# Four engines in a written order in front of the first attention of a convolution and attention network

## Chip, cores and metric

The kernel runs on one core of a Trainium2 chip. The metric is the device time of one execution in microseconds; the time before is the median of 13 executions. Engines are named as the profile names them: PE (TensorE), ACT (ScalarE), DVE (VectorE), POOL (GpSimd) and SP (SyncE, which here only issues DMAs).

## What is computed

The reference is a network of several layers on an image of 256 channels and 64 x 64 places: a windowed linear attention, a deformable convolution, a second attention, a mixture of experts, a third attention and a second mixture of experts. The change touches only the first layer. Cut to what matters:

```python
q = sigmoid(einsum(x, Wq)); k = sigmoid(einsum(x, Wk)); v = einsum(x, Wv)   # 8 heads of 32 channels
v = v / max(norm(v, axis=1), 1e-12)
Ik  = _integral(k)                       # sums over all rows above and columns to the left
Ikv = _integral(einsum('bfhw,bghw->bfghw', k, v))
for w in (1, 2, 4):                      # windows of 64, 32, 16 places
    ws = 64 // w
    wk, wkv = _box(Ik, ws), _box(Ikv, ws)          # sums in a window around each place
    attn = einsum('bdhw,bdfhw->bfhw', q, wkv)
    norm = einsum('bdhw,bdhw->bhw', q, wk)
    outs.append(attn / (norm + 1e-6))
out = einsum(concat(outs), Wout) + bout
```

`x` stands here for the image after a group normalisation (32 groups of channels); the layer's result is added to the image itself.

## The kernel before

**The stage.** `layer0` (L331) takes the image `xc`, normalises it into `y` (`group_norm`, L157) and works in two halves of 128 channels, that is four heads each. For each half three functions prepare what the attention itself (`half0`) needs: `project0` (L400), `sums0` (L445) and `norms0` (L475). The 4096 places lie in 8 blocks of 512 (8 rows of the image); a block holds 8 tiles of 8 x 8 places, and in `y`, `q` and `k` the tiles of a block follow one another.

**`project0`** makes k and then q for all 8 blocks: two matmuls of 512 columns a block into a PSUM tile `l_qk_ps` (three buffers) and a sigmoid on ACT into `l_k` or `l_q` (L408). Then, block by block, it makes keys and values with places in partitions: 8 matmuls into two tiles `l_kv_ps` (four buffers); ACT takes the sigmoid of the keys into `l_kt` (L423) and the squares of the values into `l_sq` (L425); DVE adds the squares of a head (L426) and bounds the sum (L427); ACT takes the square root (L428), for which it loads another table and then the first one again; DVE inverts it (L429) and scales the values (L432). The values go to DRAM (`l_vd`, L433). Then come the tile sums, for each 8 x 8 tile the sum of key times value: 8 matmuls of a 64 x 128 stationary and 128 columns into two `l_S_ps` tiles (they share the buffers of `l_qk_ps`), of which only the four 32 x 32 squares on the diagonal are wanted; ACT copies each square by itself into `l_S` (L443), eight copies a block.

**`sums0`** runs on POOL (all at L449) when all blocks of `l_S` are there: pairs of neighbouring tiles, `l_near` (sums of three rows of pairs), and sums over seven neighbouring tiles in columns (`l_R`) and then in rows (back into `l_S`). The results go to DRAM as `l_neard` and `l_fard`.

**`norms0`** makes the normalisers. ACT copies k into a raster `l_T` (L485), DVE takes a running sum along each row of a block (L486, with `gate` as a reset at each row's start) and then adds rows and blocks (L487), so that `l_T` holds the integral of k. For each block and window, DVE subtracts two stretches of rows (L502, `l_d`), ACT copies the left edge (L504), DVE subtracts columns (L506 and L508, `l_e`) and multiplies by q (L510, `l_prq`, three buffers); PE adds over the channels of a head (L515, `l_nrm_ps`, with `head_at`); at the end DVE adds 1e-6 and inverts (L517, L518), and the result goes to DRAM (`l_recd`).

**What sets the order.** The order of each engine's instructions in this stage is chosen by a scheduler from the dependencies and its own estimates; only in the attention that follows is PE's order the written one (`manual_schedule` with PE alone). Every engine and the SP queue work strictly in that order: an instruction that waits holds up all behind it. A tile pool gives a tag a number of buffers, and who writes a buffer waits for all readers of what it held.

**Then attention.** `vt` (values with the places of a column strip in partitions) is loaded from `l_vd` by `tall` (L375), half of it through SP's and half through ACT's queue; its space was that of the prepared stage, so it waits for the last `l_nrm_ps` matmul. `bd` (L382) are block-diagonal states, cleared by POOL and filled from `l_fard` and `l_neard` (L530). The first matmuls of attention are `l_s` (L657); they need a strip of k (`l_kc`, L551).

Of the kernel before, what the change touches and what calls it, by code (L numbers as in the profile page):

```python
# [10 lines left out]
F32 = mybir.dt.float32  # L11
# [77 lines left out]
class Net:  # L89
# [145 lines left out]
    def consts0(self, pool):  # L235
# [8 lines left out]
        self.gate = pool.tile([P, TR, HW], F32, tag="gate", name="gate")  # L244
# [86 lines left out]
    def layer0(self, xc, x, xd, done):  # L331
# [4 lines left out]
        with tc.tile_pool(name="l0", bufs=1) as pool, tc.tile_pool(name="l0d", bufs=1, space=DRAM) as dpool:  # L336
# [9 lines left out]
            with tc.tile_pool(name="l0y", bufs=1) as ypool:  # L346
                self.consts0(ypool)
# [5 lines left out]
                with (  # L353
                    tc.tile_pool(name="l0g", bufs=1) as gpool,
                    tc.tile_pool(name="l0a", bufs=2) as wp,
                    tc.tile_pool(name="l0a_ps", bufs=2, space=PSUM) as ps,
                ):
                    self.weights(ypool, ["w_qk0", "w_kv0"])
                    for hf in range(2):
                        S = gpool.tile([P, NBLK, NU, D], F32, tag="S", name="l0_S")  # L360
                        self.project0(hf, y, q[hf], k[hf], None if hf else v, vd[hf], S, wp, ps)
                        self.sums0(S, fard[hf], neard[hf], gpool)
                        self.norms0(q[hf], k[hf], recd[hf], gpool, wp, ps)
            with (
# [6 lines left out]
                def tall(hf):  # L371
                    by_rows = vd[hf].rearrange("(i b j) (h n) c -> b n i j h c", b=2, j=4, h=2)
                    for b in range(2):
                        for i in range(4):
                            (nc.sync, nc.scalar)[b].dma_start(  # L375
                                out=vt[b * HW : (b + 1) * HW, i].rearrange("p (j h) c -> p j h c", h=2), in_=by_rows[b][:, i])
# [4 lines left out]
                for b in bd[0] + bd[1]:  # L381
                    nc.gpsimd.memset(b, 0.0)  # L382
# [16 lines left out]

    def project0(self, hf, y, q, k, v, vd, S, wp, ps):  # L400

        nc, w = self.nc, self.w
        for dst, base in ((k, C), (q, 0)):
            cols = slice(base + hf * P, base + hf * P + P)
            for nb in range(NBLK):
                p = ps.tile([P, NB], F32, tag="qk", name="l0_qk_ps", bufs=3)
                self.mm(p, [(w["w_qk0"][:, kt, cols], y[:, kt, nb * NB : (nb + 1) * NB]) for kt in range(2)])
                nc.scalar.activation(dst[:, nb * NB : (nb + 1) * NB], p, AF.Sigmoid)  # L408
        cols = slice(hf * 2 * P, (hf + 1) * 2 * P)
        for nb in range(NBLK):  # L410
            ts = slice(nb * TPB, (nb + 1) * TPB)
            vb = wp.tile([P, TPB, P], F32, tag="vb", name="l0_vb") if v is None else v[:, ts, :]
            kt4 = wp.tile([P, TPB, P], F32, tag="kt", name="l0_kt")
            ss = wp.tile([P, TPB, 4], F32, tag="ss", name="l0_ss")
            sq = wp.tile([P, TPB, 4, D], F32, tag="sq", name="l0_sq")
# [12 lines left out]
            nc.scalar.activation(ss, ss, AF.Sqrt)  # L428
            nc.vector.reciprocal(ss, ss)  # L429
# [3 lines left out]
            nc.sync.dma_start(out=vd[ts].rearrange("t p c -> p t c"), in_=vb)  # L433

            sums = [ps.tile([P, TPB, P], F32, tag="qk", name="l0_S_ps", bufs=3) for _ in range(2)]
            for i in range(TPB):
                for b, p in enumerate(sums):
                    half = slice(b * HW, (b + 1) * HW)
                    self.mm(p[:, i, :], [(kt4[half, i, :], vb[half, i, :])])
            for b, p in enumerate(sums):  # L440
                for h in range(4):
                    hp = slice(h * D, (h + 1) * D)
                    nc.scalar.copy(S[hp, nb, b::2, :], p[hp, :, hp])  # L443

    def sums0(self, S, fard, neard, pool):  # L445


        nc = self.nc
        add = lambda o, a, b: nc.gpsimd.tensor_tensor(o, a, b, ALU.add)  # L449
        pairs = pool.tile([P, NBLK, 4, D], F32, tag="pairs", name="l0_pairs")  # L450
# [2280 lines left out]
```

## Time and profile before

| what | us |
|---|---|
| median of 13 runs (3566.31 to 3579.47) | 3574.62 |
| the profiled execution's own time | 3573.69 |
| its span, first to last instruction | 3571.6 |
| first projection matmul (`l_qk_ps`) starts | 34.95 |
| last addition of the first half's integral (L487) starts | 66.25 |
| last normaliser matmul (`l_nrm_ps`) of the second half starts | 274.83 |
| first attention matmul (`l_s`) starts | 294.18 |

The mean granted clock of PE is 0.946. In the profile's rows a line is given with the engine, the operation, the tile written and those read, shapes as partitions x elements, and in square brackets the idle time before it and what ended it. A matmul in 32-bit floats leaves two records, so 8 matmuls in the code are 16 in the trace. A merged row gives the time from the first of its instructions to the end of the last.

### The profile page before, as it was taken

The page shows a single profiled execution, that of the slowest core. Times are in us where ns is not written, and L with a number is a line of the kernel's source. Part 1 is how long each engine was busy: PE and PEld are TensorE (multiplying, and loading weights), DVE is VectorE, ACT ScalarE, POOL GpSimd, SP SyncE. Part 2 cuts the span into 40 slices and gives each one's busy share as a digit, 9 for nine tenths or more (in the row PEclk, how much of TensorE's full clock was granted, in tenths as well). Part 3 has the DMA queues.
Part 4 walks back from the last instruction along what each step waited for, and adds up shares of the span by engine and source line. Part 5 has one row for each costly group of instructions (what it writes and reads, how often), then busy time and mean ns, then how long its engine had stood idle before and what let it go on. Part 6 is the DMA issues. An engine that isn't in the chain of part 4 may idle for free.

```text
span 3571.6 us, 64097 instructions
## 1 busy us (share of the span) xinstructions
PE 3175.8 (89%) x24636; PEld 2355.9 (66%) x24636; DVE 2314.2 (65%) x5296; ACT 1357.8 (38%) x2681; POOL 1503.0 (42%) x1336
## 2 busy tenths in 40 slices
PE   5867999999996899797877979999999996999997
PEld 3332444444444888765665747888888885898986
DVE  6784666667764677797445566777777775555552
ACT  4553333344334666342332344222222221333331
POOL 1336777788862555443233435000000002555552
PEclk9978999999998999898878989999999997999998
DMA  1115755721115222200117854223332323555554
GB/s 68 35 42 111 175 146 152 188 70 51 51 51 174 61 74 73 56 1 1 37 41 240 258 207 154 89 97 99 99 97 88 95 89 123 184 189 210 195 200 185
DMA packets 241424, 406.87 MB, mean 114 GB/s; under 512 B 78097, under 2 KB 152594, under 8 KB 231634
## 3 DMA queue, kind: packets, MB, share of 16 engines
q1 hardware_dynamic: 212658, 345.19, 31.1%
q0 software_dynamic: 13056, 35.93, 2.6%
q10 hardware_dynamic: 15392, 21.52, 1.9%
q8 instruction: 198, 3.24, 0.4%
q14 instruction: 120, 0.98, 0.1%
HBM read 287.07 MB, written 111.30 MB: 112 GB/s over the span
## 4 chain that ended last, share of the span: by engine, by line
PE 39%; DVE 7%; issue 6%; DMA 5%; POOL 3%; ACT 2%; SPq 0%; POOLq 0%; DVEq 0%; ACTq 0%
PE a_sa_ps L2354 6%; PE f_h_ps L146 5%; PE a_oa_ps L2393 3%; PE a_ob_ps L2393 3%; PE a_oc_ps L2393 3%; DMA ys<-f_y,f_at 3%; PE a_sb_ps L2354 3%; PE f_ya_ps L146 2%; PE f_yb_ps L146 2%; POOL ys L2109 1%; PE a_od_ps L2393 1%; PE l_acc_ps L1048 1%; PE a_q_ps L146 1%; PE a_sc_ps L2354 1%; PE a_s L1544 1%
## 5 line engine op out<-in xcount | busy, mean ns | idle before, releaser
L664 ACT COPY l_sc<-l_s 128x384 f32<-128x384 f32 (+1 forms) x632 | 303.6, 532 | 469.7 <-PE l_s L657 445.9
L669 DVE TENSOR_TENSOR l_sm<-l_s,mask 128x256 f32<-128x256 f32 (+2 forms) x628 | 308.1, 551 | 95.5 <-PE l_s L657 94.6
L1922 POOL DMA_INDIRECT xs<-f_room,f_to x64 | 64.7, 1012 | 699.9 <-issue 586.9
L146 PE MATMUL f_h_ps<-f_xT,f_w 128*128 128x256 f32 x1440 | 341.2, 388 | 18.8 <-ACT f_h L2039 8.1
L146 PEld LDWEIGHTS f_h_ps<-f_xT,f_w 128*128 128x128 f32 x1440 | 262.3, 192 | 83.3 <-ACT f_h L2039 21.5
L657 PE MATMUL l_s<-l_q,l_k 32*128 32x256 f32 (+3 forms) x2944 | 272.1, 454 | 0.1
L2373 ACT ACTIVATE a_e<-a_e 128x512 f32<-128x512 f32 x256 | 155.9, 629 | 245.8 <-DVE a_e L2343 231.2
L674 POOL TENSOR_TENSOR l_sm<-l_sc,mask 128x768 f32<-128x768 f32 (+1 forms) x116 | 202.5, 1753 | 87.8 <-ACT l_sc L664 87.6
L2039 ACT ACTIVATE f_h<-f_h_ps,f_w 128x256 f32<-128x256 f32 x360 | 166.3, 470 | 187.3 <-PE f_h_ps L146 177.2
L1044 DVE TENSOR_TENSOR l_pr<-l_vk,l_w_ps 128x1280 f32<-128x1280 f32 x128 | 186.6, 1481 | 56.1 <-PE l_acc_ps L1048 38.0
L657 PEld LDWEIGHTS l_s<-l_q,l_k 32*128 32x128 f32 x2944 | 133.1, 184 | 116.2 <-issue 67.9
L1048 PE MATMUL l_acc_ps<-ident,l_pr 128*128 128x128 f32 x1600 | 198.8, 278 | 8.7 <-POOL l_pr L1039 8.5
L2109 POOL DMA_INDIRECT ys<-f_y,f_at x144 | 146.0, 1014 | 138.8 <-ACT f_y L2108 88.6
L1048 PEld LDWEIGHTS l_acc_ps<-ident,l_pr 128*128 128x128 f32 x1600 | 185.4, 144 | 15.5 <-POOL l_pr L1039 10.4
L678 POOL TENSOR_TENSOR l_sm<-l_sc,mask 128x256 f32<-128x256 f32 (+1 forms) x220 | 185.2, 871 | 23.5 <-ACT l_sc L664 22.6
L2066 POOL TENSOR_TENSOR f_wt<-f_w 128x512 f32<-128x512 f32 x72 | 89.9, 1269 | 218.3 <-PE f_ya_ps L146 206.1
L2354 PE MATMUL a_sa_ps<-a_q,a_kt 128*128 128x256 f32 x512 | 156.5, 387 | 16.4 <-DVE a_u L2359 15.4
L2358 ACT COPY a_u<-a_sa_ps 128x256 f32<-128x256 f32 x128 | 47.6, 372 | 293.5 <-PE a_sa_ps L2354 289.3
L703 PE MATMUL l_b_ps<-l_sm,l_v 128*32 128x256 f32 (+2 forms) x2176 | 154.1, 374 | 0.0
L2354 PE MATMUL a_sa_ps<-a_qt,a_kt 128*128 128x256 f32 x512 | 152.7, 380 | 0.0
L674 POOL TENSOR_TENSOR l_sm<-l_sc,mask_c 128x768 f32<-128x768 f32 (+1 forms) x64 | 120.0, 1894 | 34.6 <-ACT l_sc L664 34.1
L2354 PE MATMUL a_sb_ps<-a_qt,a_kt 128*128 128x256 f32 x512 | 131.4, 379 | 0.0
(549 smaller groups left out, 7477.6 us busy)
## 6 DMA issues: line engine op xcount, KB each, us to landing
a_kt<-a_kd SPq DMA_DIRECT2D x128, 512.0 KB
f_w<-in_f_w SPq DMA_DIRECT2D x36, 1152.0 KB
f_w<-in_f_w SPq DMA_DIRECT2D x36, 1028.0 KB
xs<-zero SPq DMA_DIRECT2D x8, 4160.0 KB
l_vk<-vt SPq DMA_DIRECT2D x180, 128.0 KB
f_x<-xs SPq DMA_DIRECT2D x72, 260.0 KB
f_w<-in_f_w SPq DMA_DIRECT2D x36, 384.0 KB
l_rcp<-l_recd SPq DMA_DIRECT2D x48, 256.0 KB
```

Source lines behind the costliest of these rows:

```text
L146: self.nc.tensor.matmul(out, lhsT, rhs, start=(i == 0), stop=(i == len(pairs) - 1))
L657: nc.tensor.matmul(s[pair, j][:, at : at + m, :], key(hp), qs[hp], start=(z == 0), stop=(z == len(pieces) - 1))
L664: nc.scalar.copy(sc[:, j], s[1, j])
L669: nc.vector.tensor_tensor(to(pair, j, kind, at), pick(s[pair, j], kind, which), mask, ALU.mult)
L674: nc.gpsimd.tensor_tensor(out[:, :, at, :], of[:, :, which, :], bc(mask, 1, 2), ALU.mult)
L678: nc.gpsimd.tensor_tensor(to(1, j, kind, at), pick(sc[:, j], kind, which), mask, ALU.mult)
L1044: nc.vector.tensor_tensor(pr, vk, bc(held["w"][:, j, dy], 3, D), ALU.mult)
L1048: nc.tensor.matmul(acc[:, m, j, :], pf[:, dx, m * P : (m + 1) * P], self.ident, is_transpose=True, start=(j == 0 and dy == 0 and dx == 0 a ...
L2039: nc.scalar.activation(h[:, m, :], q, AF.Gelu, bias=w1[:, 2 * hidden + m : 2 * hidden + m + 1])
L2109: nc.gpsimd.indirect_dma_start(out=self.ys_parts[(i % 4) * NI + k], in_=y[:, k, :], in_offset=None, out_offset=bass.IndirectOffsetOnAxis(a ...
L2354: mm = lambda out, i, right: nc.tensor.matmul(out, A[i], right, start=True, stop=True)
L2393: nc.tensor.matmul(out, vs[:, j, i, :], right, start=(j == 0 and side != 1), stop=(j == NPAIR - 1 and side != 0))
```

## The change

The three functions are replaced by one, `prep0`, called for each half, and the order of PE, DVE, ACT and POOL inside it is the written one.

- First the 8 k blocks. ACT takes the sigmoid twice out of PSUM, once straight into the raster `l_T` and once into `l_k`; the copy L485 is gone. `l_T`, `gate` and `l_d` get a column of zeros in front (65 instead of 64), so that the subtraction of columns needs no copy of a left edge; L504 is gone. Running sums and the 14 additions follow as before.
- Then, for block b: POOL subtracts rows for windows 64 and 32 (`ahead`; the one for window 16 is made by DVE); PE makes q of block b+1 and keys and values of block b; then what was left *behind* from block b-1 is done: its tile sums and their copies, its running sums on POOL, its normaliser matmuls; then DVE weighs block b by q (`weighed`) and scales its values (`values`). The weighting is written in two parts, of which the first reads the row difference directly.
- A tile sum is made of four matmuls of 64 x 32 stationary and 32 columns, one for each head, so that `l_S_ps` holds only what is wanted and ACT copies it in two pieces.
- The sums over tiles run along with the blocks: the seven neighbours in columns at once, those in rows as a running window over the last blocks. `l_fard` and `l_neard` are written after block 7.
- `vt` is loaded by column strip in 8 DMAs on each queue, strips 4 to 7 first, instead of 4. The first `bd` is cleared by DVE.

The diff, cut to its core:

```diff
-        self.gate = pool.tile([P, TR, HW], F32, tag="gate", name="gate")
+        self.gate = pool.tile([P, TR, HW + 1], F32, tag="gate", name="gate")
...
-                    for hf in range(2):
-                        S = gpool.tile([P, NBLK, NU, D], F32, tag="S", name="l0_S")
-                        self.project0(hf, y, q[hf], k[hf], None if hf else v, vd[hf], S, wp, ps)
-                        self.sums0(S, fard[hf], neard[hf], gpool)
-                        self.norms0(q[hf], k[hf], recd[hf], gpool, wp, ps)
+                    self.consts0(ypool)
+                    T = gpool.tile([P, HW + 1, HW + 1], F32, tag="T", name="l0_T")
+                    nc.gpsimd.memset(T[:, 0, :], 0.0)
+                    nc.gpsimd.memset(T[:, 1:, 0:1], 0.0)
+                    ET = mybir.EngineType
+                    with tc.manual_schedule(engines={ET.PE, ET.DVE, ET.Activation, ET.Pool}):
+                        for hf in range(2):
+                            self.prep0(hf, y, q[hf], k[hf], None if hf else v, vd[hf], fard[hf], neard[hf], recd[hf], T, gpool, wp, ps)
...
-                        for i in range(4):
-                            (nc.sync, nc.scalar)[b].dma_start(
-                                out=vt[b * HW : (b + 1) * HW, i].rearrange("p (j h) c -> p j h c", h=2), in_=by_rows[b][:, i])
+                    for u in (4, 5, 6, 7, 0, 1, 2, 3):
+                        for b in range(2):
+                            (nc.sync, nc.scalar)[b].dma_start(out=vt[b * HW : (b + 1) * HW, :, u], in_=by_rows[b][:, :, u // 2, u % 2])
...
-                    nc.gpsimd.memset(b, 0.0)
+                    (nc.vector if b is bd[0][0] else nc.gpsimd).memset(b, 0.0)
...
+        def channels(dst, nb, base, also=None):
+            p = ps.tile([P, NB], F32, tag="qk", name="l0_qk_ps", bufs=3)
+            cols = slice(base + hf * P, base + hf * P + P)
+            self.mm(p, [(w["w_qk0"][:, kt, cols], y[:, kt, blk(nb)]) for kt in range(2)])
+            if also is not None:
+                nc.scalar.activation(also, p.rearrange("p (u r c) -> p r u c", u=NU, r=TR), AF.Sigmoid)
+            nc.scalar.activation(dst[:, blk(nb)], p, AF.Sigmoid)
...
+            sums = [ps.tile([P, TPB, D], F32, tag="qk", name="l0_S_ps", bufs=3) for _ in range(2)]
             for i in range(TPB):
-                for b, p in enumerate(sums):
-                    half = slice(b * HW, (b + 1) * HW)
-                    self.mm(p[:, i, :], [(kt4[half, i, :], vb[half, i, :])])
+                for h in range(4):
+                    for b, p in enumerate(sums):
+                        half, hp = slice(b * HW, (b + 1) * HW), slice(h * D, (h + 1) * D)
+                        self.mm(p[hp, i, :], [(kt4[half, i, hp], vb[half, i, hp])])
             for b, p in enumerate(sums):
-                for h in range(4):
-                    hp = slice(h * D, (h + 1) * D)
-                    nc.scalar.copy(S[hp, nb, b::2, :], p[hp, :, hp])
+                nc.scalar.copy(S[:, nb, b::2, :], p)
...
+                if i >= ni:
+                    hi, d = d, wp.tile([P, TR, HW + 1], F32, tag="d", name="l0_d", bufs=3)
+                    sub = (nc.vector if ws == 16 else nc.gpsimd).tensor_tensor
...
+                mid = HW - 2 * half
+                if mid > 0:
+                    nc.vector.tensor_tensor(e[:, :, :mid], d[:, :, 2 * half : HW], d[:, :, :mid], ALU.subtract)
+                nc.vector.tensor_tensor(e[:, :, mid:], bc(d[:, :, HW], 2, half), d[:, :, mid : mid + half], ALU.subtract)
                 pr = wp.tile([P, NU, TR, HC], F32, tag="prq", name="l0_prq", bufs=3)
+                nc.vector.tensor_tensor(to[:, :, :ni], wide(d[:, :, half : 2 * half]), q5[:, i, :, :ni], ALU.mult)
+                nc.vector.tensor_tensor(to[:, :, ni:], wide(e), q5[:, i, :, ni:], ALU.mult)
...
+            plus(pair, a[:, 0::2], a[:, 1::2])
+            ends, two = o[:, 0:8:7], o[:, 1:7:5]
+            plus(ends, a[:, 0:5:4], a[:, 1:6:4])
+            plus(two, a[:, 2:7:4], a[:, 3:8:4])
+            plus(ends, ends, two)
+            for u in range(1, 4):
+                plus(o[:, u], o[:, u - 1], a[:, u + 3])
+                plus(o[:, 7 - u], o[:, 8 - u], a[:, 4 - u])
+            if nb > 0:
+                plus(near[:, nb], pairs[:, 0], pairs[:, 1])
...
+            if nb > 1:
+                plus(near[:, nb - 1], near[:, nb - 1], pair)
+                if nb < 7:
+                    plus(S[:, max(0, nb - 3)], S[:, max(0, nb - 4)], o)
...
+            if nb == 7:
+                plus(S[:, 7], last, o)
+                for i in range(6, 3, -1):
+                    plus(S[:, i], S[:, i + 1], R[:, i - 3])
+                nc.sync.dma_start(out=fard, in_=S)
+                nc.sync.dma_start(out=neard, in_=near)
...
+        behind = []
+        channels(q, 0, 0)
+        for nb in range(NBLK):
+            ds = ahead(nb)
+            if nb + 1 < NBLK:
+                channels(q, nb + 1, 0)
+            got = keys(nb)
+            for go in behind:
+                go()
+            prs = weighed(nb, ds)
+            vals = values(nb, *got)
+            behind = [lambda nb=nb, vals=vals: tiles(nb, *vals), lambda nb=nb: sums(nb), lambda nb=nb, prs=prs: norms(nb, prs)]
+        for go in behind:
+            go()
```

## The prediction

> **What bounds the stage now.** I read the page first, then busy time by stage, then the timeline of the stage that the change rewrites. The chain that ended last names no line of this stage among its large shares, so it is read from the timeline.
>
> From the page:
>
> ```profile
> span 3571.6 us, 64097 instructions
> PE 3175.8 (89%) x24636; PEld 2355.9 (66%) x24636; DVE 2314.2 (65%) x5296; ACT 1357.8 (38%) x2681; POOL 1503.0 (42%) x1336
> ```
>
> Busy time by stage (stretch, length, then PE, weight load, DVE, ACT and POOL busy with instruction counts, granted clock, DMA share, GB/s):
>
> ```profile
> 67.00:126.00 59.00, 51.74 (x289) 34.51 (x288) 30.49 (x72) 50.82 (x131) 6.26 (x4) 1.00 0.13 36
> 126.00:165.00 39.00, 32.60 (x62) 9.00 (x61) 35.14 (x45) 9.09 (x22) 22.38 (x20) 0.91 0.10 40
> 165.00:234.00 69.00, 55.11 (x289) 35.64 (x288) 53.00 (x105) 54.92 (x139) 1.26 (x1) 0.95 0.12 34
> 234.00:276.00 42.00, 20.02 (x26) 2.00 (x24) 37.66 (x45) 5.06 (x17) 26.79 (x22) 0.63 0.09 38
> 276.00:294.00 18.00, 0.00 (x0) 0.00 (x0) 3.95 (x2) 0.00 (x0) 3.04 (x5) 0.55 0.92 195
> ```
>
> The bound changes hands. In the first and third rows keys and values run (ACT 86% busy, DVE half idle); in the second and fourth normalisers run (DVE 90%; in the fourth PE is 48% busy at a clock of 0.63). The last row waits for DMA. Inside a key/value block the timeline shows why it takes 6.05 us:
>
> ```profile
> 87.00 0.17 DVE L427 TENSOR_SCALAR l_ss<-l_ss 128x16 f32<-128x16 f32 x1
> 88.26 1.28 ACT L428 ACT_TABLE_LOAD   x1
> ...
> 89.79 1.28 ACT L423 ACT_TABLE_LOAD   x1
> 89.81 0.25 DVE L429 RECIPROCAL l_ss<-l_ss 128x16 f32<-128x16 f32 x1 [2.63 <-ACT l_ss L428]
> 90.16 0.76 DVE L432 TENSOR_TENSOR l_v<-l_kv_ps,l_ss 128x256 f32<-128x256 f32 x2
> ...
> 90.73 1.25 PE L146 MATMUL l_S_ps<-l_v,l_kt 64*128 64x128 f32 x16 [1.15 <-DVE l_v L432]
> ```
>
> DVE waits 2.63 us for a square root that stands behind eight copies of tile sums and a table load. And when POOL adds beside DVE, this happens:
>
> ```profile
> 131.74 5.77 POOL L449 TENSOR_TENSOR l_R<-l_R,l_S 128x256 f32<-128x256 f32 x6
> 132.25 0.82 DVE L508 TENSOR_TENSOR l_e<-l_d 128x248 f32<-128x248 f32 x1
> ...
> 133.20 1.00 DVE L510 TENSOR_TENSOR l_prq<-l_e,l_q 128x512 f32<-128x512 f32 x1
> ...
> 149.16 0.69 DVE L510 TENSOR_TENSOR l_prq<-l_e,l_q 128x512 f32<-128x512 f32 x1
> ```
>
> Six POOL adds and six DVE operations alternate one to one: the same L510 takes 1.00 us beside POOL and 0.69 without. This is the price to watch, for the change puts POOL adds beside DVE in every block.
>
> **The new order, step by step.** Times are from the span's start; DVE operations in a row start 0.08 us closer than their durations.
>
> *Integral of k, half 0.* Before, the twelfth k matmul ends at 42.3 (row at 34.95, 7.38 us). Five more blocks of 4 records at 0.43 us: 50.9. One sigmoid (0.60, now straight from PSUM into T; it replaces the 0.62 copy L485), one scan (1.20), a hand-over of 0.1: 52.7. Then 14 dependent additions L487 at 0.72 (520 instead of 512 elements): 62.9. Before, the last was done at 66.9.
>
> *First block.* Reduce 0.72, maximum 0.12, weighting, reciprocal and two products 1.1 (89.81 to 90.92). Weighting by start-to-start times (256 elements 0.34, 128 0.20, 64 0.13, 384 0.47, 448 0.54): window 64: 3 x 0.34 = 1.0; window 32: 0.34+0.20+0.20+0.47 = 1.2; window 16: 0.47+0.13+0.13+0.54 = 1.3, and from block 1 on its row difference 0.72. Sum 3.5 without, 4.2 with. Block 0: 5.5 us, taken as 5.7 for hand-overs.
>
> *Other blocks.* A new wait closes a loop. PE does q(b+1), keys(b), then tile sums(b-1), normaliser matmuls(b-1). DVE's first weighting of block b needs a buffer of l_prq (three of them) that the normaliser matmuls of b-1 have read; those stand behind tile sums(b-1) on PE, which wait for values(b-1) of DVE. Per turn, from the end of the values: tile sums end 0.8 later (64 records; the nearest row, L690 with 64 records of 32 columns, takes 1.10; they start after the first of two products), normaliser matmuls 1.06 (six records at 110.08), rest of the weighting 3.9, collisions 2.0, reciprocal and products 1.1: **8.9 us**.
>
> Behind PE's wait stand q(b+1), keys(b) and so the ACT chain. They have slack: PE's own work is 4 x 0.43 + 3.72 + 1.1 + 1.06 = 7.6 us a block. ACT's is about 5.0 (two table loads 2.56, five activations 1.6, square root 0.22, two copies of tile sums 0.5 in place of eight at 2.14), and the square root now has the 4 us of weighting to hide in. If that cover went, it would be the old 2.63 us a block.
>
> *Collisions.* POOL's running sums are 13 adds a block, after the two copies, that is just as weighting resumes; behind them on POOL stand the row differences of the next block (10 a half), which fall on DVE's reduce and products, operations with at most one SBUF input. POOL adds take 0.48 (128 elements, L2335 and its neighbours), 0.68 (256), 1.16 (512), hence by the slope 0.36 at 64 and 0.30 at 32. In the rows above a pair takes 0.96; DVE's share is 0.44, so POOL's is 0.52 of its 0.68: 0.16 is hidden. Eleven adds met: 3 x 0.20 + 6 x 0.14 + 2 x 0.32 = 2.0. Ends: 0, if POOL runs in DVE's wait, and 3.9 (all of 3 x 0.36 + 6 x 0.30 + 2 x 0.48).
> The Trainium skill (SBUF — State Buffer, "Who interferes with whom") says that a DVE instruction with two SBUF inputs and a GpSimd instruction that reads SBUF exclude each other for the whole instruction, which speaks against this change. By it the collisions would be 3.9 and the forecast 27 us later; the alternating rows agree in kind and are 0.16 us milder, so I keep 2.0.
>
> *Tile sums.* 64 records of 32 columns replace 16 of 128 (1.25 us). Bounds: 1.10 (L690, 17 ns apart) and 5.0 (the old rows' 78 ns each). I take 1.1: L690 is nearest in stationary width and count.
> The Trainium skill (TensorEngine Tiling (Array Packing), "Instruction Overhead") gives each matmul some 60 cycles and warns against narrowing what is already small. L690 at 17 ns apart says that different array tiles share such a cost; no run here shows this exact tile.
>
> *Sum.* A half is 5.7 + 7 x 8.9 = 68.0. Half 0: 62.9 + 68.0 = 130.9, last tile sums and normalisers 1.9: 132.8. Half 1 starts only there, since PE is in order: 8 k blocks x 1.72 = 13.8, sigmoid, scan and hand-over 1.9, additions 10.1: 158.6. Half 0's reciprocal of 3.35 us on DVE lies beside the k blocks. Then 68.0 and 1.9: **228.5**, against 275.9 before (last L515 row, 274.83 + 1.05). Gain so far 47.4.
>
> *Hand-over to attention.* Before: 275.9 to the first l_s matmul at 294.2, 18.3 us. Now SP has fard and neard of half 1 ahead of its vt loads, and they wait for POOL: copies done at 228.0, 16 adds 7.0 (12 as above, four of 256): 235.0. ACT's half of vt moves meanwhile. Issue times alone (recd and states 0.7, 8 vt at 0.57, w_out 0.63, four bd 2.58, kc 0.66) and the landing of kc (3.1) give 247.3. By bytes: 3.8 MB are left (neard 0.5, fard 1, recd 0.2, vt 1, w_out 0.75, bd 0.13, kc 0.25) where 3.3 MB took 15.2 us plus 3.1: 255.6. I take **252**: nearer to the bytes. So 5 to 6 us of the gain go back. Edits at nothing: the first bd memset on DVE (about 0.5 us; it waits for transfers out of the space that it takes, and behind it on DVE stand the first l_sm products, which need the first l_s matmul anyway); the pads of T and gate; vt of half 1 in eight pieces a queue, with the far jobs of half 0 to hide in, or 0.57 us each on ACT if that cover goes.
>
> Net: 294.2 - 252 = 42 us. The profiled execution took 3573.69 us (2.1 us around its span; median of the runs 3574.62): 3573.7 - 42 = **3532**. Later stages keep their order on every engine.
>
> **Rivals.**
> A, PE is the bound: POOL's adds slip into DVE's wait. The loop falls to PE's 7.6: 14 blocks x 1.3 = 18 less, 3514. For: POOL's small adds leave DVE gaps. Against: sums and weighting are released together.
> B, POOL holds DVE for whole adds: 14 x 1.9 = 27 more, 3559. For: L502 at 1.75 against 0.69 beside larger POOL adds. Against: the 0.16 above.
> C, slower than before: the 64 small matmuls are not shared among array tiles. At the old 78 ns each, tile sums take 5.0 and stand in the loop: 16 x 3.9 = 62 more, 3594. It decides from 42/16 = 2.6 us extra, 58 ns a record. For: the old tile sums' rows. Against: L690.
> D, the order doesn't come out as written, or gains are lost at the hand-over: within 0.2%, 3572. Against: the built order shows PE, DVE, ACT and POOL as written.
>
> **Numbers.** Forecast 0.56, A 0.13, B 0.17, C 0.10, D 0.04. A measurement of this kernel tells 0.2% (7 us) from no change. Range 3509 (A with the hand-over at 247) to 3564 (B with it at 256). Faster 0.85 (forecast, A, most of B), same 0.04, slower 0.11.
>
> **What would show it.** Right: last scan at 52 to 53 and the first reduce at 63; blocks 8.9 us apart; l_nrm matmuls behind tile sums and DVE waiting for them 0.5 to 1 us a block; DVE's L502-like operations stretched while POOL runs; nrm of half 1 done near 228; first l_s matmul near 252. Wrong: tile sums over 2.5 us, blocks over 11, a granted clock below 0.85 with PE 80% busy, or ACT's square root late again.

## The result and the profile after

The changed kernel takes **3521.07 us** (median of 7 runs, 3513.49 to 3530.48) against 3573.98 (31 runs) for the kernel before; the ratio is 0.9855 (95% interval 0.9843 to 0.9867), 53 us less. The forecast was 3532, 42 us less. The profiled execution took 3525.29 us.

Up to the first matmul of attention (`l_s`) the forecast holds almost to the microsecond: 251.49 us where 252 was forecast. The 10 us that are missing from the forecast come after it: the first output projection (`l_x_ps`) starts at 352.7 instead of 405.5, 52.8 us earlier. In this one profile 4 us of that are lost again later (the span is 48.4 shorter); the medians, with 53, do not show this loss.

From the page after:

```profile
span 3523.2 us, 65631 instructions
PE 3133.8 (89%) x25404; PEld 2346.2 (67%) x25404; DVE 2303.5 (65%) x5325; ACT 1318.9 (37%) x2537; POOL 1567.6 (44%) x1523
```

DVE and PE are hardly less busy than before, POOL is busier. What went is waiting, as busy time by stage shows (columns as in the rows of before: stretch, length, PE, weight load, DVE, ACT, POOL, granted clock, DMA share, GB/s):

```profile
35.00:63.00 28.00, 27.74 (x76) 15.04 (x76) 20.70 (x26) 17.18 (x30) 0.30 (x2) 1.00 0.00 0
63.00:130.00 67.00, 47.45 (x640) 28.67 (x640) 61.15 (x136) 34.54 (x70) 53.44 (x99) 0.85 0.11 29
130.00:160.00 30.00, 29.45 (x143) 15.46 (x122) 24.28 (x25) 14.10 (x26) 7.36 (x18) 0.93 0.19 68
160.00:227.00 67.00, 48.02 (x673) 29.20 (x676) 60.37 (x135) 34.81 (x72) 54.45 (x100) 0.84 0.10 29
227.00:245.00 18.00, 1.56 (x6) 0.00 (x0) 4.95 (x3) 0.16 (x1) 8.55 (x21) 0.50 0.92 230
```

The eight blocks of a half are the second and the fourth row. DVE is busy for 91% of them (it was 52% in the key/value stage before), POOL for 80%, PE for 71% at a clock of 0.85. DVE is nearest its limit, but these are means over a half; what holds a single block is read from the timeline.

The timeline of the changed kernel, first in block 0, where POOL does nothing, then in two blocks of the second half of the row (start, duration, engine, line, operation; in brackets the idle time before it and who ended it):

```profile
63.16 0.68 DVE L443 TENSOR_REDUCE l_ss<-l_sq 128x16 f32<-128x512 f32 x1
63.87 0.17 DVE L444 TENSOR_SCALAR l_ss<-l_ss 128x16 f32<-128x16 f32 x1
63.95 0.42 DVE L497 TENSOR_TENSOR l_e<-l_T 128x256 f32<-128x256 f32 x1
64.29 0.42 DVE L500 TENSOR_TENSOR l_prq<-l_T,l_q 128x256 f32<-128x256 f32 x1
...
68.47 0.68 DVE L443 TENSOR_REDUCE l_ss<-l_sq 128x16 f32<-128x512 f32 x1
...
71.12 0.56 DVE L500 TENSOR_TENSOR l_prq<-l_T,l_q 128x256 f32<-128x256 f32 x1 [1.45 <-PE l_nrm_ps L509]
...
93.07 0.75 PE L146 MATMUL l_S_ps<-l_v,l_kt 64*32 64x32 f32 x64 [1.08 <-DVE l_v L454]
...
94.20 0.22 ACT L445 ACTIVATE l_ss<-l_ss 128x16 f32<-128x16 f32 x1 [0.22 <-DVE l_ss L444]
...
95.32 1.49 DVE L497 TENSOR_TENSOR l_e<-l_d 128x256 f32<-128x256 f32 x1 [1.15 <-POOL l_d L478]
...
101.58 0.24 DVE L451 RECIPROCAL l_ss<-l_ss 128x16 f32<-128x16 f32 x1
...
103.24 1.02 DVE L444 TENSOR_SCALAR l_ss<-l_ss 128x16 f32<-128x16 f32 x1
104.27 1.49 DVE L497 TENSOR_TENSOR l_e<-l_d 128x256 f32<-128x256 f32 x1
105.67 0.67 DVE L500 TENSOR_TENSOR l_prq<-l_d,l_q 128x256 f32<-128x256 f32 x1
```

The reader is to see four things. The square root (L445) waits 0.22 us at 94.20, and in other blocks up to 4.2, but always for DVE's own maximum (L444); DVE's reciprocal (at 101.58) waits for it in no block, where it waited 2.63 before. Tile sums take 0.75 us for 64 records. The wait that was forecast, DVE for normaliser matmuls, is there once (at 71.12, block 1). From block 4 on there is another: DVE waits for POOL's row differences `l_d` (1.15 us in blocks 4 and 7), or what runs on DVE beside them is drawn out (L444 1.02 instead of 0.17, L497 1.49 instead of 0.42). In block 5 the long L444 costs nothing by itself: L497 at 104.27 reads the row difference on which POOL works from 103.03 to 104.23, so with a short L444 DVE would have waited for it, as at 95.32. POOL's own timeline tells why:

```profile
94.10 2.43 POOL L478 TENSOR_TENSOR l_d<-l_T 128x520 f32<-128x520 f32 x2
96.49 0.64 POOL L520 TENSOR_TENSOR l_pairs<-l_S 128x128 f32<-128x128 f32 x1
97.09 0.96 POOL L520 TENSOR_TENSOR l_R<-l_S 128x64 f32<-128x64 f32 x2
98.13 0.38 POOL L520 TENSOR_TENSOR l_R<-l_R 128x64 f32<-128x64 f32 x1
98.59 2.59 POOL L520 TENSOR_TENSOR l_R<-l_R,l_S 128x32 f32<-128x32 f32 x6
101.14 0.84 POOL L520 TENSOR_TENSOR l_near<-l_pairs 128x128 f32<-128x128 f32 x1
101.94 0.45 POOL L520 TENSOR_TENSOR l_near<-l_near,l_pairs 128x128 f32<-128x128 f32 x1
102.35 0.73 POOL L520 TENSOR_TENSOR l_S<-l_S,l_R 128x256 f32<-128x256 f32 x1
103.03 2.44 POOL L478 TENSOR_TENSOR l_d<-l_T 128x520 f32<-128x520 f32 x2
```

There is no gap, and none from 87.95 to 131.05: from one pair of row differences to the next POOL needs 8.93 us, and that is the block. The six small additions take 2.59 us here; at 228.79, with DVE out of the way, the same six take 1.30.

### The profile page after: what moved, and what is told of

Same layout as the page of the kernel before. It is cut to its first block, busy times and chain, and to the rows that moved or that the text cites. A ratio compares the mean times of both kernels' runs of the same rounds, so it can differ in the third digit from the quotient of the medians.

```text
span 3523.2 us, 65631 instructions
## 1 busy us (share of the span) xinstructions
PE 3133.8 (89%) x25404; PEld 2346.2 (67%) x25404; DVE 2303.5 (65%) x5325; ACT 1318.9 (37%) x2537; POOL 1567.6 (44%) x1523
```

## Experiments

The theory after these rows: the alternation of weighting with keys and values gives the gain; the pace of a block is set by three engines that are near 9 us each (POOL alone in blocks 4 to 7, the forecast's loop only in the first ones); the 10 us behind the first `l_s` are a wait of the kernel before that the cut of the `vt` loads took away. The rival is the forecast as it stood: one loop through DVE and PE at 8.9 us, with POOL only as a collision.

The chips differ by up to 2% in the time of the whole, so each kernel is compared by its ratio to the kernel before on its own chip, and by two landmarks of its trace. The changed kernel's landmarks agree on two chips within 0.4 us. But vt_half1_whole, whose code up to the first `l_s` is that of the changed kernel, has it 1.8 us later and block 1 of half 0 0.65 us longer, so less than 2 us at the first `l_s` and less than 0.7 us in the sum say nothing. Intervals are from one start of tile sums to the next in half 0; the sum is over all seven. In half 1 the sum is steadier: 61.1 in changed, after_again, vt_half1_whole, later_loads and early_k alike.

| kernel | ratio (95%) | first `l_s` | first `l_x_ps` | intervals of blocks, half 0 | sum |
|---|---|---|---|---|---|
| before | 1 | 294.2 | 405.5 | | |
| changed | 0.9855 (0.9843 to 0.9867) | 251.5 | 352.7 | 9.00 7.53 8.18 9.36 8.93 8.86 9.50 | 61.4 |
| after_again | 0.9853 (0.9832 to 0.9873) | 251.1 | 352.5 | 9.09 7.52 8.17 9.35 8.95 8.84 9.51 | 61.4 |
| vt_half1_whole | 0.9878 (0.9856 to 0.9900) | 253.3 | 363.2 | 9.65 7.52 8.17 9.35 8.96 8.84 9.51 | 62.0 |
| no_sums | one run, 3499.4 | 239.6 | 340.7 | 8.59 7.05 7.64 8.64 8.51 8.50 7.51 | 56.4 |
| diff_dve | 0.9830 (0.9812 to 0.9849) | 251.8 | 353.5 | 9.60 8.13 8.08 8.78 8.79 8.78 8.78 | 60.9 |
| apart | 0.9970 (0.9960 to 0.9980) | 295.4 | 396.7 | | |
| wide_tiles | 0.9870 (0.9854 to 0.9887) | 258.2 | 359.4 | 9.75 7.45 9.07 9.55 8.73 9.47 9.73 | 63.8 |
| no_written_order | 0.9850 (0.9834 to 0.9866) | 254.1 | 355.3 | (irregular, 10 to 10.8 at the end) | |
| later_loads | 0.9840 (0.9824 to 0.9857) | 248.6 | 353.3 | as changed | |
| early_k | 0.9847 (0.9832 to 0.9862) | 250.2 | 352.4 | 9.37 7.52 8.16 9.34 8.96 8.83 9.53 | 61.7 |
| grouped | 0.9859 (0.9840 to 0.9878) | 253.2 | 355.2 | 8.94 9.01 7.23 9.80 8.48 9.99 9.30 | 62.8 |
| best | 0.9829 (0.9815 to 0.9844) | 241.1 | 343.8 | 7.11 8.29 7.04 9.27 7.95 10.66 9.02 | 59.3 |
| norms_first | 0.9821 (0.9798 to 0.9844) | 244.0 | 345.3 | 7.11 7.05 7.92 9.35 8.95 8.84 9.81 | 59.0 |

### The loads of half 1's values in whole pieces again (vt_half1_whole)

```diff
 def tall(hf):
+    if hf == 1:
+        for b in range(2):
+            for i in range(4):
+                (nc.sync, nc.scalar)[b].dma_start(out=vt[b*HW:(b+1)*HW, i]..., in_=by_rows[b][:, i])
+        return
```

> The changed kernel, but the loads of half 1's tall values (l_vt) are again four whole pieces per queue, cut by strip number, instead of eight pieces cut by unit. The trace of the changed kernel has the first l_s matmul 42.7 us earlier than before, but the first l_x_ps matmul 52.8 us earlier: 10 us that no term of the prediction has. Theory: they come from a stall that went. Before, TensorE idles 6.9 us at 374.5 (l_b_ps matmuls wait for DVE's l_o, which waits for the load of l_far, issued on SyncE only at 377.6, behind a store of l_od that stands behind the whole vt loads), and the clock is 0.74 in the stretch after. By it this kernel shows a TensorE wait of 6 to 7 us before the first l_b_ps matmuls again and is 8 to 10 us slower than the changed kernel. Rival: the extra gain is spread over the attention or is a difference of profiles; then this kernel is within 3 us of the changed one.

In the kernel before, DVE's timeline has it standing still at the change from the far jobs to the rest:

```profile
380.67 0.69 DVE L722 TENSOR_TENSOR l_o<-l_a_ps,l_far 128x512 f32<-128x512 f32 x1 [6.94 <-DMA l_far<-l_od]
```

Its SP timeline has what DVE waits for, `l_far`, issued late, behind the `vt` loads and a store of `l_od`:

```profile
366.65 1.75 SPq L375 DMA_DIRECT2D l_vt<-l_vd  x2
368.66 1.97 SPq L565 DMA_DIRECT2D l_od<-l_o  x1
377.56 4.14 SPq L576 DMA_DIRECT2D l_far<-l_od  x3
```

In vt_half1_whole the same comes back. Its waits of PE between 245 and 420 (in total, times, longest):

```profile
PE l_b_ps L745 <- DVE l_o L777: 5.8, 1, 5.8
```

Its SP timeline:

```profile
325.41 1.55 SPq L378 DMA_DIRECT2D l_vt<-l_vd  x2
327.51 0.56 SPq L620 DMA_DIRECT2D l_od<-l_o  x1
335.54 0.82 SPq L631 DMA_DIRECT2D l_far<-l_od  x2
```

A whole piece holds all eight column strips, so each has to wait until the last far job has read its part of `vt`; then all four of SP are issued within 7 us (319.73 to 326.96), ahead of the last store of `l_od` (moved by the same queue), and `l_far` is read back late, 8.0 us behind that store instead of 3.2. Cut by strip, each piece goes as soon as its own far job is done. From the first `l_s` to the first `l_x_ps` this kernel needs 109.9 us, the changed one 101.2: 8.7 us, of which 5.1 are the wait itself (5.8 against 0.7). In the wait's stretch from 335 to 345 the granted clock is 0.66; that accounts for the rest only by argument. In all other kernels of the table with the cut loads, later_loads apart, the same stretch is 101.1 to 102.7 us; in the kernel before it is 111.3. The theory holds: 8.7 of the 10 us are shown to be the cut of these loads. By the ratio the whole is 8 us longer, with intervals that overlap.

### Keys and values apart from weighting (apart)

```diff
 for nb in range(NBLK):
-    ds = ahead(nb)
     ...keys(nb); what is behind; values(nb)
+for nb in range(NBLK):
+    norms(nb, weighed(nb, ahead(nb)))
```

> The changed kernel with keys and values of all eight blocks first and the normalisers of all eight blocks after them, in the same half, the same written order otherwise, so that only their alternation is undone. Theory: the gain is that ACT's and TensorE's block work lies beside DVE's weighting. Apart, a half is eight blocks at TensorE's 6.2 us (1.7 + 3.7 + 0.8) and eight weightings at 4.4 to 5, 85 to 90 us instead of 67: 34 to 45 us more in all. Rival: the gain comes from the shorter work itself (sigmoid from PSUM, no copies of tile sums, square root not behind them), and the alternation gives back in collisions what it hides; then this kernel is at most 12 us slower.

Busy time by stage of apart, half 0's keys and values, then its normalisers:

```profile
63.00:107.00 44.00, 38.79 (x632) 27.93 (x630) 17.05 (x44) 34.27 (x72) 24.97 (x79) 0.94 0.16 44
107.00:150.00 43.00, 25.95 (x39) 3.18 (x40) 38.17 (x78) 0.21 (x2) 27.10 (x38) 0.74 0.11 43
```

The first stretch is PE's and ACT's with DVE 39% busy, the second DVE's with ACT idle: the two patterns of the kernel before. The first `l_s` comes 44 us later than in the changed kernel, and the ratio rises by 0.0115, 41 us. With the shorter work but without the alternation, 0.3% of the time is gained instead of 1.45%, and even that lies behind the first `l_s`, where the cut of the `vt` loads acts: the first `l_s` itself, at 295.4, is no earlier than in the kernel before (294.2). The theory of the alternation is shown.

### Running sums left out (no_sums)

```diff
 def sums(nb):
+    if nb == 7:
+        nc.gpsimd.memset(near, 0.0)
+        ...store near and S as they are
+    return
```

> The changed kernel with all running sums on POOL left out (l_near is set to zero and l_S is stored as the tile sums are), so that its output lacks the running sums. Theory from the trace of the changed kernel: in blocks 4 to 7 POOL works back to back (row differences 2.4 us, sums 6.6 us a block: 9.0, the block's own 8.9), DVE waits for POOL's row differences and is stretched by the rest. Without the sums DVE needs about 6.3 us a block and TensorE 7.1 at full clock, so late blocks fall to 7.1 to 7.7, a half from 67 to 57 to 59 us, the normalisers of half 1 end near 210 instead of 228.6, and the first l_s matmul comes 20 to 25 us earlier, since the seven us of last sums ahead of the transfers are gone too. The forecast's own view (collisions 2.0 a block, and otherwise the loop of 6.9) gives the same floor by TensorE's 7.6: 18 us. Rival: TensorE with its clock of 0.85 in this stage is the bound; then a half falls by less than 4 us.

The intervals sum to 56.4 instead of 61.4: 5 us a half, half of what was expected. The first `l_s` comes 12 us earlier, not 20 to 25. The waits of its DVE between 63 and 131 (in total, times, longest) name what takes POOL's place:

```profile
DVE l_prq L500 <- PE l_nrm_ps L509: 4.1, 5, 1.4
DVE l_ss L443 <- ACT l_sq L442: 2.7, 2, 1.7
```

Five waits for normaliser matmuls where the changed kernel has one: the forecast's loop, at about 8.5 us, lies directly under POOL's pace. And POOL's row differences still draw DVE out (at 103.84 an L496 takes 1.42, at 106.06 an L478 1.69 us). So all thirteen additions a block were worth 0.7 us a block, because the next two limits follow at once.

### Row differences on DVE (diff_dve)

```diff
-sub = (nc.vector if ws == 16 else nc.gpsimd).tensor_tensor
+sub = nc.vector.tensor_tensor
```

> The changed kernel with all row differences (l_d) on DVE instead of two of three on POOL. Theory (POOL's chain paces blocks 4 to 7): POOL's chain falls from 9.0 to 6.6 us; DVE loses the wait of 1.15 and the stretch of the maximum (0.9 where it shows) and pays two subtractions of 0.72, and some of these now meet sums: late blocks 8.4 to 8.9, blocks 2 and 3 of a half some 0.7 longer, in all from 4 us less to 3 us more. Rival (the forecast's loop: DVE is the bound and POOL only stretches it): ten subtractions a half at 0.72 are added to DVE, 14 us more.

Late blocks take 8.78 instead of 8.93, blocks 2 and 3 together 0.5 more, the sum 60.9 instead of 61.4 (in half 1 it is 61.1 in both); the landmarks stay within 1 us. The rival (14 us more) falls, and with it the view that DVE's own work sets the pace of the changed kernel; here it is DVE that has no gap in blocks 4 to 7. The ratio is 0.0025 under that of the changed kernel; since both landmarks say that the stage is no shorter and the intervals overlap, no gain is claimed. The kernel gives the collisions cleanly, since DVE waits for nothing in blocks 4 to 7: its operations undisturbed are 5.31 us (63.16 to 68.47 above) and three differences of 0.72, 7.47 in all, so POOL's thirteen additions cost **1.3 us a block**.

### Normaliser matmuls ahead of tile sums on PE (norms_first)

```diff
-behind = [tiles(nb, *vals), sums(nb), norms(nb, prs)]
+behind = [norms(nb, prs), tiles(nb, *vals), sums(nb)]
```

> The changed kernel with one edit on TensorE's order: the normaliser matmuls of a block ahead of its tile sums instead of behind them. This takes the forecast's loop apart: DVE's first weighting of the next block no longer waits for tile sums and normaliser matmuls after the values. By the forecast's loop a block loses the 0.8 + 1.06 that stand there, unless DVE's own 6.9 to 7.6 bind first: 1.3 us a block, 18 us in all. Theory from the traces since (POOL back to back with row differences and sums at 9.0 us in blocks 4 to 7; the predicted wait shows in one block of eight): late blocks stay at 8.8 to 9.4, only the first blocks gain 0.5 to 1.5 each, 62 us from first to last tile sums become 59.5 to 61.5, and the whole is 2 to 5 us less than the changed kernel.

This is the cleanest test of the forecast's loop, since it opens it and changes nothing else. Blocks 1 to 3 fall by 1.9, 0.5 and 0.3 us; the late ones stay (9.35, 8.95, 8.84), and the last is 0.3 longer. The waits of its DVE between 63 and 131:

```profile
DVE l_e L497 <- POOL l_d L478: 2.3, 2, 1.2
DVE l_ss L443 <- ACT l_sq L442: 1.4, 1, 1.4
```

The wait for `l_nrm_ps` in a block is gone, the wait for POOL stays: the forecast's loop bound the first blocks of a half, POOL the others. In its PE timeline the matmuls now run while the values are made:

```profile
106.69 1.05 PE L509 MATMUL l_nrm_ps<-l_prq,head_at 128*32 128x512 f32 x4
108.62 1.05 PE L509 MATMUL l_nrm_ps<-l_prq,head_at 128*32 128x512 f32 x2 [0.87 <-DVE l_prq L501]
109.59 0.76 PE L146 MATMUL l_S_ps<-l_v,l_kt 64*32 64x32 f32 x64
```

The landmarks come 7.5 and 7.4 us earlier, more than the expected 2 to 5: the blocks give 2.4 us in half 0 and 2.0 in half 1. Besides, the last normaliser matmuls no longer stand at the end of a half behind its last values: half 1's k projections start 0.7 us after half 0's last tile sums (128.92) instead of 2.7 (132.39), and four of SP's eight `vt` loads are issued from 220.47 on, ahead of the store of `l_neard`, where the changed kernel has all eight at 235.22.

### Wide tile sums again (wide_tiles)

```diff
-4 heads: self.mm(p[hp, i, :], [(kt4[half, i, hp], vb[half, i, hp])])
+self.mm(p[:, i, :], [(kt4[half, i, :], vb[half, i, :])])
...
-nc.scalar.copy(S[:, nb, b::2, :], p)
+for h in range(4): nc.scalar.copy(S[hp, nb, b::2, :], p[hp, :, hp])
```

> The changed kernel, but tile sums as before: 16 records of 64x128 and eight copies out of them, in place of 64 records of 64x32 and two copies. The narrow form took 0.75 us a block (12 ns a record) where the wide one took 1.25, and two copies 0.42 us on ACT where eight took 2.14. Theory (three engines bind near 8.9 us a block, and ACT is not among them: 4.4 of 8 us busy): only TensorE's 0.5 us a block shows, and of the copies what exceeds ACT's waits for TensorE (0.7 to 1.6 us a block); 3 to 12 us slower than the changed kernel. Rival (the narrow tiles are what made the alternation possible, since the copies hold the square root): 2.2 us a block on the path, 35 us slower. Other rival: narrow tiles cost more than they give in a busy TensorE; then not slower.

6.7 to 7.1 us later at both landmarks, the ratio 0.0017 up (6 us): the theory's range, not the 35 of the first rival. The narrow form is a part of the gain, not what makes it possible.

### The order left to the planner (no_written_order), with the base (after_again)

```diff
-with tc.manual_schedule(engines={ET.PE, ET.DVE, ET.Activation, ET.Pool}):
+if True:
```

> The changed kernel with the order of this stage left to the planner on all engines instead of written by hand on four. The built order then has on ACT the tile-sum copies ahead of the square root, on TensorE four key/value blocks' parts between normaliser matmuls, and k of half 1 drawn ahead of the last key/value blocks of half 0. Theory (the loop of values, tile sums and normaliser matmuls sets the pace): the square root waits for copies and these for values, 1 to 2 us a block, 15 to 30 us slower; less what the earlier k of half 1 gives, up to 13 us. Rival: the engines settle to the same pace in any order, because each is near its own 8 to 9 us a block; then within 5 us.

> The changed kernel itself, as the base for the three others on this chip. Both theories: the ratio to before is within 0.3% of 0.9855, the first l_s matmul within 2 us of 251.5 and the first l_x_ps matmul within 2 us of 352.7.

The ratio is that of the changed kernel (0.9850 against 0.9853), the landmarks 2.8 to 3.0 us later. Late intervals are 9.9 to 10.8, as the theory says, and half 0's last tile sums start at 136.3 instead of 130.0. Half 1 adds nothing to that (last tile sums at 232.4 instead of 226.1), and at the hand-over 3 us come back. Two rows of its PE timeline, around the change of halves:

```profile
136.33 0.76 PE L146 MATMUL l_S_ps<-l_v,l_kt 64*32 64x32 f32 x64
...
161.24 0.36 PE L146 MATMUL l_S_ps<-l_vb,l_kt 64*32 64x32 f32 x32 [1.18 <-DVE l_vb L454]
```

From half 0's last tile sums to half 1's first it is 24.9 us, where the base has 35.1. That is not the doing of k projections drawn into half 0, as the text put on record for this kernel has it: they start at 137.02, behind those last tile sums. DVE scales the first block's values (160.67) ahead of the last additions of the integral, which end at 164.8. In sum 3 us are lost, not 15 and more: the rival's number, though not its reason, since late blocks are 1 us and more longer. The whole times do not tell the two orders apart. Writing the order by hand gave little by itself; the functions cut by block give the gain under either order.

### Fewer bytes ahead of attention (later_loads)

```diff
-tall(0); self.weights(wop, ["w_out0"])
+tall(0, (4, 5, 6, 7))
+# after the first l_s jobs: tall(0, (0, 1, 2, 3)) and the weights
```

> The changed kernel with what attention doesn't need first taken off the hand-over: of the tall values only the units 4 to 7 are loaded ahead, units 0 to 3 and the output weights are loaded after the first l_s jobs have been issued. Theory (the hand-over is bound by bytes: in the changed kernel DMA is 92% busy at 230 GB/s from 227 to 245): 1.05 + 0.79 MB less ahead of the first kc, 8.0 us by bytes; by issue times SP has 235.0 + 0.7 + 4 x 0.6 + 2.6 + 0.66 and 3.1 of landing, 244.5. The first l_s matmul comes at 243.5 to 245 instead of 251.5, and the whole is 6 to 8 us shorter. Rival (the stores of fard and their reading back set it, whatever else is moved): less than 2 us.

Missed: 2.5 us at the first `l_s`, nothing left at the first `l_x_ps`. SP's queue of later_loads:

```profile
234.49 0.33 SPq L547 DMA_DIRECT2D l_fard<-l_S  x1
235.56 0.32 SPq L567 DMA_DIRECT2D l_recd<-l_rec  x1
235.97 3.66 SPq L377 DMA_DIRECT2D l_vt<-l_vd  x4
241.88 2.57 SPq L578 DMA_DIRECT2D l_bd<-l_fard  x4
244.50 0.66 SPq L599 DMA_DIRECT2D l_kc<-l_k  x1
245.20 2.70 SPq L377 DMA_DIRECT2D l_vt<-l_vd  x4
```

Between 241 and 246 DMA is 58% busy at 93 GB/s here, where the base on the same chip has it full (1.07, 173 GB/s). So bytes do not set the first `l_s` once fewer are moved: issuing does (four `vt`, four `bd` and `kc` fill SP from 235.97 to 245.16 with a gap of 2.2 us ahead of `bd`), and the landing. The gap is a wait for DVE's clearing of `bd` (1.2 us) and for the stores of `l_recd` (0.6) and `l_fard` (0.3), so the rival has little part in it. In the base SP waits 2.2 us for a `vt` load ahead of the output weights, which are put off here. ACT's queue kept all eight of its `vt` loads early (228.97 to 240.57), so that less was put off than meant. What was put off is then in the way of the next jobs: first `l_s` to first `l_x_ps` takes 104.7 us, 3.3 more than in the base.

### k of half 1 drawn forward (early_k)

```diff
 for i in range(NBLK):                      # k blocks of half 1
+    if i == 3: what was behind in half 0
     channels(k, i, C, ...)
```

> The changed kernel, but the last block's tile sums, running sums and normaliser matmuls of half 0 are issued after the first three k projections of half 1 instead of ahead of them. In the changed kernel TensorE waits 6.8 us for the last values of a half with nothing else to do, while the order left to the planner drew k of half 1 into that place and began half 1's blocks 24 us after half 0's last tile sums instead of 34. Theory (TensorE's order binds at the change of halves): three k blocks of 1.72 us go into the wait, so the first tile sums of half 1 come 5 us earlier (160 instead of 165.1), and so does the first l_s matmul (246 instead of 251.1 to 251.5). Rival: the rows of l_T that the new k needs are still read, or DVE's scans and additions set the start; then less than 1.5 us.

The text above takes it that the planner drew k of half 1 forward; the rows of no_written_order do not show that. What early_k tries is PE's wait at the end of a half. From half 0's first tile sums to half 1's it is 93.5 us instead of 96.5: 3 of the 5 us. DVE's timeline of early_k shows what took the rest:

```profile
131.13 4.61 DVE L428 TENSOR_TENSOR_SCAN l_T<-gate,l_T 128x520 f32<-128x520 f32 x3
135.66 0.66 DVE L572 TENSOR_SCALAR l_rec<-l_nrm_ps 96x512 f32<-96x512 f32 x1
136.35 3.35 DVE L573 RECIPROCAL l_rec<-l_rec 96x512 f32<-96x512 f32 x1
139.62 5.72 DVE L428 TENSOR_TENSOR_SCAN l_T<-gate,l_T 128x520 f32<-128x520 f32 x5
145.38 12.31 DVE L421 TENSOR_TENSOR l_T<-l_T 128x520 f32<-128x520 f32 x14
```

Here DVE is without a gap. The reciprocal of 3.35 us, which lay beside k projections, is now on its path, and the fourteen additions take 12.31 instead of 10.27 us, since they now meet POOL's last sums of half 0 (until 151.2). The first `l_s` is 0.9 us earlier, which is less than kernels of the same code differ by there.

### Sums of two blocks at a time (grouped), and all together (best)

```diff
-a, o = S[:, nb], R[:, nb]                       # one block
+a, r = S[:, nb-1:nb+1], R[:, nb-1:nb+1]         # blocks 0 to 5: two, after the second; row differences on DVE
```

> All row differences on DVE (as in diff_dve), and POOL's running sums of blocks 0 to 5 made for two blocks at a time, so that nine additions of 64 to 256 elements take the place of eighteen of 32 to 128. In diff_dve a late block is 8.79 us, DVE is busy throughout, and its own operations undisturbed come to 7.46, so 1.3 us a block are collisions (the forecast had 2.0). Theory (DVE pays by POOL's time on the port): POOL's adds fall from 6.6 us a block to about 4.4, collisions to 0.9; blocks 8.3 to 8.5 on the mean, 62 us from first to last tile sums become 59 to 60.5, in all 3 to 6 us less than diff_dve. Rival (no_sums: without any sum late blocks were still 8.5, by the wait for normaliser matmuls and by POOL's row differences): the loop holds them at 8.6, and less than 2 us come.

Missed: the sum is 62.8, 1.9 more than diff_dve (2.3 more in half 1). POOL's busy time from 63 to 130 falls from 44.3 to 32.1 us, but what is left lies in every second block: those take 9.0 to 10.0 us, the light ones 7.2 to 8.9. The likely reason, that a heavy block is held by POOL and DVE and a light one by PE, so that less work gives nothing once it is uneven, is argued from these intervals and not tried apart.

> Early k, row differences on DVE, sums of two blocks at a time, and on TensorE the normaliser matmuls of a block ahead of its tile sums, so that they run while the values are made. Theory (each of DVE, POOL and TensorE is held near 8.5 to 9 us a block, so they have to be cut together): collisions fall to 0.9, the wait for l_nrm is gone and TensorE has 1.06 us less behind the values; late blocks 8.0 to 8.4, 57 to 59 us from first to last tile sums, twice 3 to 5, and 5 from early k: the first l_s matmul at 237 to 241 and 9 to 14 us less than the changed kernel in all (ratio 0.981 to 0.983). Rival: the parts don't add up, as with diff_dve, where DVE took over what POOL gave up: 5 us less at most (0.984 and above).

best adds early k and normaliser matmuls first: first `l_s` at 241.1 (10 us earlier than in the changed kernel), first `l_x_ps` at 343.8 (8.7 to 8.9 earlier), ratio 0.9829 (0.9815 to 0.9844). That is the lower edge of the theory's 9 to 14, but not by way of its blocks of 8.0 to 8.4: the late ones take 8.0 to 10.7. A half's sum of 59.3 is no better than norms_first alone gives with its one line. Both beat the changed kernel by the landmarks; between the two the measurement does not decide.

## Why the forecast was right, and where it was not

**First half's integral, block 0, change of halves: right.** First reduce at 63.16 (62.9 forecast), block 0 5.4 us (5.7), half 1's first reduce at 159.53 (158.6).

**Tile sums: right in kind, smaller.** 0.75 us (1.1 taken, bounds 1.10 and 5.0): 12 ns a record. The rival that made the kernel slower needed 58 ns. The row that the 1.1 was taken from, L690, moves 64 columns a record (its shapes are 128*32 and 128x64), not 32 as the forecast has it; that may be part of the difference. The Trainium skill (TensorEngine Tiling (Array Packing), "Instruction Overhead") counts some 60 cycles for each matmul and warns of narrowing what is small. These rows do not settle that price: the page gives it in cycles for a matmul, and a matmul of the code is two records here, 23 ns together. What they show is that the narrow form is the shorter one, and wide_tiles the slower kernel.

**Blocks: 8.8 us on the mean where 8.9 was forecast, for a partly wrong reason.** That the two numbers agree is in part luck. The step that failed is "A new wait closes a loop" as the pace of every block. The loop binds block 1 (1.45 us of wait) and, by what norms_first gains there, a little of blocks 2 and 3; norms_first opens it and gains 2.0 to 2.4 us a half, not 1.3 a block. From block 4 on POOL works without a gap. The forecast had the parts of this on its page, 13 additions and two row differences, but never added them up for POOL. At the forecast's own prices, for POOL undisturbed, that would have been about 7.4 us a block (5.0 for the additions, 2.4 for the differences), under the loop's 8.9; beside DVE the additions take 6.5 instead, and POOL needs 8.9. Rival B had POOL holding DVE, not POOL as an engine that is full.

**Collisions: too small as a sum, and wrong in its parts.** In a late block of the changed kernel DVE's own work is 7.47 less two differences of 0.72, that is 6.03, of 8.93: 2.9 us are lost, where 2.0 were forecast. L444 (0.95 too long, start to start) and L497 (1.06) lose 2.0 us beside POOL's two row differences; the rest, 0.9, is the sums. The forecast gave the sums 2.0 and the row differences nothing, because they "fall on DVE's reduce and products, operations with at most one SBUF input". L444, the maximum, stands between them. It has one SBUF input and was still drawn out from 0.17 to 1.02. The Trainium skill (SBUF — State Buffer, "Who interferes with whom") names tensor_scalar among the operations that can take the shared ports in a fast mode, and says that the engine that comes second blocks for the whole instruction; L444 is such an operation, and with 1.02 beside a row difference of 1.2 the row agrees. The forecast had used the same section for two-input operations only. That the fast mode is what holds L444 was not tried by itself.

**Change to attention: right number, wrong account.** 251.49 against 252; `fard` is issued at 234.16 (235.0 forecast). later_loads shows that the 252 does not follow from bytes alone: with fewer ahead it was 248.6, not 244. (The change also swaps the order of the two tile pools `l0g` and `l0a`; no run takes that back by itself.)

**After it: the miss.** "Edits at nothing: ... vt of half 1 in eight pieces a queue" was costed by what issuing it costs. What it takes away was on record in the trace of before: a wait of PE of 6.9 us at 374.5 for `l_far`, behind these loads. vt_half1_whole puts it at 8.7 us with the clock after it, most of the difference between 42 and 53.

## What to carry to other kernels

When work of several engines is laid side by side, add up every engine's own time per turn, the lightly used one's with its stretched durations too; the largest of these sums is a floor of the turn. When several are close, taking work off one gains little (here a tenth of what the sums weighed on POOL), and the next gain is a matter of order (one line on PE gave 7 us). A moved or cut transfer is priced at the place where it stood as well as at its new one: look there for a wait that ends with it. A gain that comes before a hand-over can be lost in it, so measure at a landmark behind it.

## Not expected of the hardware

- 64 matmul records (32 matmuls of the code) of a 64 x 32 stationary and 32 columns take 0.75 us, 12 ns each; 16 of 64 x 128 and 128 columns 1.25.
- A row difference on POOL (128x520, 1.2 us) holds a DVE tensor_scalar of 16 elements a partition for 1.02 us (0.17 alone); in block 3, where both start at 85.92, L444 takes 1.31 us and the row difference 1.29. Six small POOL additions take 2.59 us beside DVE and 1.30 alone, while DVE loses 1.3 us a block to all thirteen (diff_dve): each engine pays a part.
- PE's clock falls where it waits and works by turns: in the first half of the changed kernel six normaliser matmuls take 1.93 us, at a granted clock of 0.50, where PE had waited 3.5 us or more just before (at 69.17, 120.94 and 130.53), and 1.06, at 1.00, where it had waited 1.1 or less. Over that half the granted clock is 0.85 at 71% busy, but 0.92 in norms_first, where PE is 85% busy.
